# Layer 0's scores of two key tiles taken together: four float32 products, then the four float32r position products

## The chip, the cores and the metric

The kernel runs on one core of a Trainium2 chip. Its engines are TensorE (PE in the profile; its weight loads are shown apart as PEld), VectorE (DVE), ScalarE (ACT), GpSimd (POOL) and SyncE (SP, which only issues DMAs). Each works through its own instructions in the order in which they stand in its queue, and waits for the others through semaphores. The metric is the device time in microseconds of one execution.

## The reference, cut to what matters

Eight images of 32 x 32 points with 384 channels go through two layers. Layer 0 is an attention over the 1024 points of an image, with 6 heads of 64 channels and with positions relative in height and width added to the scores; layer 1 is a causal attention with one head of 384 channels and a feed-forward part with binarized weights. The change touches the scores of layer 0:

```python
attn = jnp.einsum('bqd,bkd->bqk', q * SCALE, k)
rel_h = jnp.einsum('bhwc,hkc->bhwk', r_q, Rh)
rel_w = jnp.einsum('bhwc,wkc->bhwk', r_q, Rw)
attn = attn.reshape(b * NH, h, w, h, w) + rel_h[:, :, :, :, None] + rel_w[:, :, :, None, :]
attn = attn.reshape(b * NH, hw, hw)
attn = jax.nn.softmax(attn, axis=-1)
out = jnp.einsum('bqk,bkd->bqd', attn, v)
...
return out @ proj_w + proj_b
```

## The kernel before

The images are worked through one after another (`ORDER`; one of the three images without a feed-forward part comes first). For an image, layer 0 makes queries, keys and values and tables of relative positions; `attend0_fast` does the attention; layer 1 follows, and in five of the eight images the feed-forward part.

In `attend0_fast` the loop runs over the 3 head pairs `p` and the 2 halves of 512 queries: 6 groups an image, 48 in all. A group goes over 8 tiles of 128 keys. The two heads of a pair (`par` 0 and 1) lie on partitions 0 to 63 and 64 to 127, so that their products use different halves of the array's rows.

- `scores(p, c, half)` takes one key tile: for each head a float32 product of keys and queries (L909) starts the sum in a PSUM bank, and a float32r product of a pattern of ones (`unit`) with the positions `r` (L913) ends it. First come the two heads' L909, then the two heads' L913. Then ScalarE takes the exponential of each bank (L920) into a page `pr0`, both heads side by side.
- A plain float32 product shows in the trace as two records, a float32r one as one; so L909 has 1536 records for 768 products, L913 768 for 768.
- `add_up` sums the eight pages of a group on VectorE (L925 for the first two, L927 for the rest); `values` multiplies probabilities and values on TensorE (L935), both heads into one bank on different columns of the array; ScalarE copies that bank to `oT` (L1007) except in the last group.
- `over_tiles` reduces the sums (L944, L946, the tile `few`). In most groups the totals then go through a DMA (`gathered`, L954 and L958) and come back a group later, where `reciprocals` takes them (L974, L976). In an image's last group (and in the first image's last two) `reciprocals` adds up across partitions with a small product on TensorE (L969) at once. What follows for the last group: L976, `widened` (L983, L984), the scaling of `oT` (L1017 for the group before, L1020 for the last one), and the projections (L1026, then L524).
- After the first half of a head pair, `later(p + 1, ...)` prepares the positions of the next one: two casts on ScalarE (L784) queued behind the group's last exponential, two subtractions on VectorE (L794) behind the last sum, and DMAs into `r` (L800) from SyncE and GpSimd.

What sets the order: instructions are placed by a scheduler that keeps data dependences and, among ready ones, mostly the order of the program. `behind_last()` puts each call's products behind `last_matmul`, the last product of the call before, on TensorE's queue; it makes no engine wait for another. A score tile is one of the 8 PSUM banks of the pool `ps_o`, taken in turn: a bank is free again when the exponential that reads it is done. Pages come from a pool of 12. L829 puts the last values of layer 0 in place before the first group of an image and L1362 is the first product of the feed-forward part.

Of the kernel before, what the change touches and what calls it, by code (L numbers as in the profile page):

```python
# [14 lines left out]
AF = mybir.ActivationFunctionType  # L15
# [4 lines left out]
P = 128  # L20
B, H, W, C = 8, 32, 32, 384
T = H * W
NJ = T // P
# [68 lines left out]
def conv_attn_hybrid(  # L92
# [19 lines left out]
    nc = tc.nc  # L112
# [144 lines left out]
    unit = const.tile([P, 2, HB, WB], F32R, name="unit")  # L257
# [51 lines left out]
    def layer1_forms(pools, raw, s):  # L309
        weight_forms(pools, nc.gpsimd, raw[:, ts(s, NC * C)].rearrange("p (k o) -> p k o", k=NC), s, w1f)  # L310
# [110 lines left out]
    def stages(pools):  # L421
# [151 lines left out]
        def behind_of(ins):  # L573
            return contextlib.nullcontext() if ins is None else tc.issue_after(ins)
# [318 lines left out]
        def attend0_fast(residual, b, q, k, r, v, later):  # L893
# [4 lines left out]
            rows = (slice(0, HD), slice(HD, P))  # L898
            last_exp, last_matmul, last_few = [None], [None], [None]

            def behind_last():
                return tc.issue_after(last_matmul[0]) if last_matmul[0] is not None else contextlib.nullcontext()

            def scores(p, c, half):

                sc = [pools.o_tile(f"s0_{b}_{p}_{c}_{half}_{par}") for par in range(2)]
                with behind_last():
                    for par in range(2):
                        nc.tensor.matmul(  # L909
                            sc[par], k[rows[par], p, ts(c, P)], q[rows[par], p, ts(half, 512)], start=True, stop=False  # L910
                        )
                    for par in range(2):
                        last_matmul[0] = nc.tensor.matmul(  # L913
                            sc[par], unit[rows[par], c // 2 % 2].rearrange("i h w -> i (h w)"),
                            r(2 * (c // 4) + c % 2, p)[rows[par], ts(half, 512)], start=False, stop=True,
                        ).ins
                pr = pools.page(f"pr0_{b}_{p}_{c}_{half}")
                for par in range(2):
                    with behind_of(exp_loaded[0]):
                        last_exp[0] = nc.scalar.activation(pr[:, ts(par, 512)], sc[par], AF.Exp).ins  # L920
                return pr

            def add_up(p, half, prs):
                total = pools.page(f"sum0_{b}_{p}_{half}")
                adds = [nc.vector.tensor_tensor(total, prs[0], prs[1], ALU.add).ins]  # L925
                for pr in prs[2:]:
                    adds.append(nc.vector.tensor_tensor(total, total, pr, ALU.add).ins)  # L927
                return total, adds

            def values(p, half, prs):  # L930
                av = pools.o_tile(f"av0_{b}_{p}_{half}")
                with behind_last():
                    for c, pr in enumerate(prs):
                        for par in range(2):
                            last_matmul[0] = nc.tensor.matmul(  # L935
                                av[ts(par, HD), :], v[:, c, ts(2 * p + par, HD)], pr[:, ts(par, 512)],
                                start=(c == 0), stop=(c == NJ - 1),
                            ).ins
                return av

            def over_tiles(p, half, total):

                tr = pools.page(f"tr0_{b}_{p}_{half}")
                nc.vector.transpose(tr, total)  # L944
                few = pools.small.tile([P, 2, 16], F32, tag="few", bufs=2, name=f"few_{b}_{p}_{half}")
                last_few[0] = nc.vector.tensor_reduce(  # L946
                    few, tr.rearrange("p (a n i) -> p a n i", a=2, i=32), AX.X, ALU.add
                ).ins
                return few

            def gathered(p, half, few):

                kept = store.tile([P, 32], F32, tag="few", bufs=2, name=f"{pools.path}_few_{b}_{p}_{half}")
                nc.sync.dma_start(out=kept, in_=few.rearrange("p a n -> p (a n)"))  # L954
                parts = pools.small.tile([P, 4, 16], F32, tag="parts", bufs=2, name=f"parts_{b}_{p}_{half}")
                at = kept[0:1, 0:1]
                for i in range(4):
                    nc.sync.dma_start(  # L958
                        out=parts[ts(i, 32)],
                        in_=bass.AP(at.tensor, at.offset + i // 2 * 16, [[32, 32], [32 * 32, 4], [1, 16]]),  # L960
                    )
                return parts

            def reciprocals(p, half, few, parts=None):
                if parts is None:
                    den = pools.o_tile(f"den0_{b}_{p}_{half}")[:, :16]
                    with behind_last():
                        for par in range(2):
                            last_matmul[0] = nc.tensor.matmul(  # L969
                                den[ts(par, HD)], fold.rearrange("p a i -> p (a i)"), few[:, par, :], start=True, stop=True  # L970
                            ).ins
                else:
                    den = pools.small.tile([P, 16], F32, tag="den0", bufs=2, name=f"den0_{b}_{p}_{half}")
                    nc.vector.tensor_reduce(den, parts.rearrange("p a n -> p n a"), AX.X, ALU.add)  # L974
                rt = pools.small.tile([P, 16], F32, tag="rt0", bufs=2, name=f"rt0_{b}_{p}_{half}")
                nc.vector.reciprocal(rt, den)  # L976
                check(den, rt, b * PER_IMAGE + 2 * p + half)
                return rt

            def widened(p, half, rt):  # L980
                room = pools.page(f"wide0_{b}_{p}_{half}")
                wide, rb = room[:, :512], room[:, 512:]
                nc.vector.tensor_copy(wide.rearrange("p (n i) -> p n i", i=32), rt.unsqueeze(2).to_broadcast([P, 16, 32]))  # L983
                nc.vector.transpose(rb, wide)  # L984
                return rb

            xt, waiting = None, None
            for p, half in itertools.product(range(NPAIR), range(2)):
                t, last = ts(half, 512), (p, half) == (NPAIR - 1, 1)
                prs = [scores(p, c, half) for c in range(NJ)]  # L990
                if b == ORDER[0] and (p, half) == (0, 0):
                    with tc.issue_after(last_row[0]):
                        layer1_forms(pools, raw1[0], 1)
                if b == ORDER[0] and (p, half) == (2, 0):
                    signs.append(binarize(pools))
                    next(signs[0])
                total, adds = add_up(p, half, prs)
                if waiting is not None:
                    p0, t0 = waiting[0], ts(waiting[1], 512)
                    with tc.issue_after(adds[4 if last else 5]):  # L1000
                        rt = reciprocals(*waiting)
                    if not last:
                        rb = widened(p0, waiting[1], rt)
                        nc.gpsimd.tensor_tensor(oT[:, p0, t0], oT[:, p0, t0], rb, ALU.mult)
                av = values(p, half, prs)
                if not last:
                    nc.scalar.copy(oT[:, p, t], av)  # L1007
                if (p, half) == (1, 0):
                    xt = residual()
                if half == 0 and p + 1 < NPAIR:  # L1010
                    later(p + 1, last_exp[0], adds[-1])
                few = over_tiles(p, half, total)
                at_once = last or (b == ORDER[0] and p == NPAIR - 1)
                if last:
                    with tc.issue_after(last_few[0]):
                        rb = widened(p0, waiting[1], rt)
                    nc.vector.tensor_tensor(oT[:, p0, t0], oT[:, p0, t0], rb, ALU.mult)  # L1017
                waiting = (p, half, few, None if at_once else gathered(p, half, few))
# [522 lines left out]
    with ExitStack() as scope:  # L1541
        pools = Pools(scope, tc, "f")
# [42 lines left out]
```

## Time and profile before

| what | value |
|---|---|
| median of the runs | 2267.55 us (2267.29 to 2268.35, 3 runs) |
| the profiled execution | 2271.02 us |
| its span, first to last instruction | 2269.2 us |
| granted clock of TensorE, mean | 0.999 |
| L909 MATMUL, float32 scores | 1536 records, busy 400.6 us |
| L913 MATMUL, float32r positions | 768 records, busy 310.0 us |
| L920, exponentials on ScalarE | 768, busy 412.4 us, mean 595 ns |
| L925 and L927, sums on VectorE | 336, busy 430.2 us |
| L935 MATMUL, values | 1536 records, busy 340.2 us |

The ends of products in the trace are modelled, and a product that is issued early shows a long record; the busy times of L909 and L913 therefore overlap. What a product costs is better read from the distance between starts, or from the chain of waits, in which each stretch of time is given to one line. Shares of the span in that chain: L909 15%, L935 15%, L913 4%.

### The profile page before, as it was taken

To read this page: it belongs to the slowest core of one execution; us is meant where nothing else is said; L and a number is where in the kernel's file an instruction comes from. 1 tells how busy PE (TensorE), PEld (TensorE's weight loads), DVE (VectorE), ACT (ScalarE), POOL (GpSimd) and SP (SyncE) were. 2 spreads that over 40 slices of the span, in tenths; PEclk is the share of its full clock that TensorE was granted. 3 is DMA by queue.
4 is the path that set the end of the run, shared out by engine and by line. 5 is a ranking of instruction groups with operands and counts; after the bars stand their busy time and mean duration, and the time that the engine had idled before them with its cause. 6 is when DMAs were issued, how large, how long until landed. Compare 5 with 4: busy or idle time off the path is not lost.

```text
span 2269.2 us, 30149 instructions
## 1 busy us (share of the span) xinstructions
PE 2257.0 (99%) x10597; PEld 1387.8 (61%) x10597; DVE 1633.2 (72%) x2746; ACT 1208.3 (53%) x2181; POOL 527.2 (23%) x696
## 2 busy tenths in 40 slices
PE   9999999999999999999999999999999999999998
PEld 4547554768645677547685475874477754755475
DVE  6898578875888548886468884588864788727882
ACT  4654266337664457654476543767444766317541
POOL 7512222230131401312102313013040131221310
PEclk9999999999999999999999999999999999999999
DMA  6530562140740205520308202074102372016200
GB/s 192 146 93 28 159 139 55 47 163 29 150 104 29 73 40 120 127 65 1 112 30 186 67 29 108 21 153 111 31 5 107 73 170 60 10 47 153 56 1 30
DMA packets 182048, 188.50 MB, mean 83 GB/s; under 512 B 138763, under 2 KB 151488, under 8 KB 179072
## 3 DMA queue, kind: packets, MB, share of 16 engines
q1 hardware_dynamic: 163680, 115.80, 20.9%
q0 software_dynamic: 17376, 69.30, 9.8%
q8 instruction: 87, 1.43, 0.3%
q10 hardware_dynamic: 832, 1.38, 0.2%
q14 instruction: 73, 0.60, 0.1%
HBM read 84.52 MB, written 51.56 MB: 60 GB/s over the span
## 4 chain that ended last, share of the span: by engine, by line
PE 99%; DVE 0%; DMA 0%; SPq 0%; issue 0%; ACT 0%
PE f_s L909 15%; PE f_av L935 15%; PE f_av L1218 8%; PE f_s L1204 8%; PE f_y L1412 7%; PE f_y L1362 7%; PE f_qk L578 6%; PE f_s L913 4%; PE f_pr_A L578 4%; PE f_pr_B L578 3%; PE f_pj L1026 3%; PE f_pj L524 3%; PE f_rel L578 2%; PE f_pr_1v_A L578 2%; PE f_pr_1q_A L578 2%; PE f_pr_1v_B L578 2%
## 5 line engine op out<-in xcount | busy, mean ns | idle before, releaser
L920 ACT ACTIVATE f_pr<-f_s 128x512 f32<-128x512 f32 x768 | 412.4, 595 | 40.8 <-PE f_s L913 36.3
L909 PE MATMUL f_s<-f_q,f_k 64*128 64x512 f32 x1536 | 400.6, 595 | 2.4 <-DVE f_v L829 2.4
L927 DVE TENSOR_TENSOR f_sum<-f_sum,f_pr 128x1024 f32<-128x1024 f32 x288 | 368.0, 1278 | 25.9
L935 PE MATMUL f_av<-f_pr,f_v 128*64 128x512 f32 x1536 | 340.2, 595 | 0.0
L913 PE MATMUL f_s<-f_r,unit 64*128 64x512 f32 x768 | 310.0, 792 | 0.0
L935 PEld LDWEIGHTS f_av<-f_pr,f_v 128*64 128x64 f32 x1536 | 106.0, 137 | 218.3 <-issue 191.9
L909 PEld LDWEIGHTS f_s<-f_q,f_k 64*128 64x128 f32 x1536 | 148.0, 186 | 127.0 <-issue 66.5
L1204 PE MATMUL f_s<-f_q,f_lnT 128*128 128x512 f32 (+3 forms) x576 | 198.3, 488 | 0.0
L1218 PE MATMUL f_av<-f_v,f_pr 128*128 128x385 f32 (+1 forms) x576 | 195.4, 486 | 0.0
L800 POOL DMA_DIRECT2D f_r<-f_far x192 | 102.2, 535 | 389.9 <-DVE f_far L794 175.7
L1218 PEld LDWEIGHTS f_av<-f_v,f_pr 128*128 128x128 f32 x576 | 108.1, 190 | 77.0 <-issue 11.5
L1213 ACT ACTIVATE f_pr<-f_s 128x512 f32<-128x512 f32 (+3 forms) x96 | 47.0, 491 | 203.1 <-DVE f_s L1209 160.2
L1204 PEld LDWEIGHTS f_s<-f_q,f_lnT 128*128 128x128 f32 x576 | 100.7, 190 | 70.0 <-issue 46.9
L1373 DVE TENSOR_REDUCE am<-f_h 128x1 f32<-128x1024 f32 (+2 forms) x80 | 71.6, 946 | 95.6 <-ACT f_h L1366 95.6
L1366 ACT ACTIVATE f_h<-f_y,biases 128x256 f32<-128x256 f32 x240 | 100.8, 471 | 66.8 <-PE f_y L1362 66.8
L913 PEld LDWEIGHTS f_s<-f_r,unit 64*128 64x128 f32 x768 | 76.3, 187 | 88.7 <-issue 88.5
L578 PE MATMUL f_qk<-f_gnT,wq_sb 128*128 128x512 f32 x288 | 127.9, 595 | 0.0
L1412 PE MATMUL f_y<-f_w2a,f_hilo 128*128 128x384 f32 x640 | 127.2, 341 | 0.0
L1007 ACT COPY f_oT<-f_av 128x512 f32<-128x512 f32 x40 | 23.5, 587 | 190.4 <-PE f_av L935 190.4
L1412 PEld LDWEIGHTS f_y<-f_w2a,f_hilo 128*128 128x128 f32 x640 | 112.5, 188 | 3.8 <-issue 1.4
L925 DVE TENSOR_TENSOR f_sum<-f_pr,f_pr 128x1024 f32<-128x1024 f32 x48 | 62.2, 1295 | 71.8 <-ACT f_pr L920 71.8
L1316 POOL PARTITION_ALL_REDUCE qa<-qg x10 | 3.7, 367 | 459.1 <-DVE qg L1314 459.1
(286 smaller groups left out, 4189.2 us busy)
## 6 DMA issues: line engine op xcount, KB each, us to landing
f_far<-f_far SPq DMA_DIRECT2D x48, 512.0 KB, 4.6
f_r<-f_far SPq DMA_DIRECT2D x192, 128.0 KB, 3.0
f_r<-f_far POOLq DMA_DIRECT2D x192, 128.0 KB, 4.5
f_far<-f_far SPq DMA_DIRECT2D x192, 64.0 KB, 4.7
f_x<-in_x SPq DMA_DIRECT2D x32, 384.0 KB, 4.7
f_gnT<-in_xT SPq DMA_DIRECT2D x21, 512.0 KB, 4.8
f_w1a<-w1s POOLq DMA_DIRECT2D x5, 1536.0 KB, 6.6
f_w2a<-w2s POOLq DMA_DIRECT2D x5, 1536.0 KB, 8.2
```

Of the source, the lines that this page charges most:

```text
L578: last_product[0] = nc.tensor.matmul(*args, **kw).ins
L800: put = (nc.gpsimd if i else nc.sync).dma_start(out=r(part, p).bitcast(F32).rearrange("(m i) t -> i m t", i=4)[2 * i + d], in_=pages[i][ts ...
L909: nc.tensor.matmul(sc[par], k[rows[par], p, ts(c, P)], q[rows[par], p, ts(half, 512)], start=True, stop=False)
L913: last_matmul[0] = nc.tensor.matmul(sc[par], unit[rows[par], c // 2 % 2].rearrange("i h w -> i (h w)"), r(2 * (c // 4) + c % 2, p)[rows[pa ...
L920: last_exp[0] = nc.scalar.activation(pr[:, ts(par, 512)], sc[par], AF.Exp).ins
L927: adds.append(nc.vector.tensor_tensor(total, total, pr, ALU.add).ins)
L935: last_matmul[0] = nc.tensor.matmul(av[ts(par, HD), :], v[:, c, ts(2 * p + par, HD)], pr[:, ts(par, 512)], start=(c == 0), stop=(c == NJ - 1),
L1204: last_score[0] = nc.tensor.matmul(sc[:, lo:], xT[:, c // 4, k, ts(c % 4, P)], q[:, half, k, lo:], start=(k == 0), stop=(k == NC - 1),).ins
L1218: made = nc.tensor.matmul(av, prs[c][:, ts(j - c, P)], what(c), start=(c == 0), stop=(c == j)).ins
L1362: nc.tensor.matmul(ps, w1k[i // 2][:, ts(m, P)], xs[i % 2][:, half, i // 2, :], start=(i == 0), stop=(i == 2 * NC - 1))
L1366: nc.scalar.activation(pairs[i][:, m, :, :], ps[:, ts(i % 2, 256)].rearrange("p (j q) -> p j q", j=2), AF.Identity, bias=b1_sb[:, m : m + 1],)
L1412: nc.tensor.matmul(ps[:, :C], h, w, start=(i == 0), stop=(i == len(products) - 1))
```

## The change

`scores` takes two key tiles at a time. It issues the float32 products of both tiles and both heads, then the float32r products of both, then the four exponentials in the order in which they stood before. Banks, pages and exponentials are the same in number and order; the products of one pair of tiles stand in another order on TensorE's queue, and a pair's four banks and two pages are asked for together.

```diff
-            def scores(p, c, half):
+            def scores(p, cs, half):
-                sc = [pools.o_tile(f"s0_{b}_{p}_{c}_{half}_{par}") for par in range(2)]
+                sc = {(c, par): pools.o_tile(f"s0_{b}_{p}_{c}_{half}_{par}") for c in cs for par in range(2)}
                 with behind_last():
-                    for par in range(2):
+                    for c, par in sc:
                         nc.tensor.matmul(
-                            sc[par], k[rows[par], p, ts(c, P)], q[rows[par], p, ts(half, 512)], start=True, stop=False
+                            sc[c, par], k[rows[par], p, ts(c, P)], q[rows[par], p, ts(half, 512)], start=True, stop=False
                         )
-                    for par in range(2):
+                    for c, par in sc:
                         last_matmul[0] = nc.tensor.matmul(
-                            sc[par], unit[rows[par], c // 2 % 2].rearrange("i h w -> i (h w)"),
+                            sc[c, par], unit[rows[par], c // 2 % 2].rearrange("i h w -> i (h w)"),
                             r(2 * (c // 4) + c % 2, p)[rows[par], ts(half, 512)], start=False, stop=True,
                         ).ins
-                pr = pools.page(f"pr0_{b}_{p}_{c}_{half}")
-                for par in range(2):
+                prs = [pools.page(f"pr0_{b}_{p}_{c}_{half}") for c in cs]
+                for c, par in sc:
                     with behind_of(exp_loaded[0]):
-                        last_exp[0] = nc.scalar.activation(pr[:, ts(par, 512)], sc[par], AF.Exp).ins
-                return pr
+                        last_exp[0] = nc.scalar.activation(prs[c - cs[0]][:, ts(par, 512)], sc[c, par], AF.Exp).ins
+                return prs
...
-                prs = [scores(p, c, half) for c in range(NJ)]
+                prs = [pr for c in range(0, NJ, 2) for pr in scores(p, (c, c + 1), half)]
```

## The prediction

> **What bounds the kernel now.** I read the page first: busy shares and the chain that ended last.
>
> ```profile
> PE 2257.0 (99%) x10597; PEld 1387.8 (61%) x10597; DVE 1633.2 (72%) x2746; ACT 1208.3 (53%) x2181; POOL 527.2 (23%) x696
> PE 99%; DVE 0%; DMA 0%; SPq 0%; issue 0%; ACT 0%
> L920 ACT ACTIVATE f_pr<-f_s 128x512 f32<-128x512 f32 x768 | 412.4, 595 | 40.8 <-PE f_s L913 36.3
> ```
>
> TensorE (PE) is the chain from end to end, so only two things count: how long a product holds the array, and whether the array is ever made to wait. The exponentials (L920) wait for TensorE, not the reverse. Next I read the chain of waits in order of time, at the end of a scores group (image 0, last head pair and half) and in the first feed-forward product of the same image; the columns are start, length, what, and how many records. A plain float32 product is two records.
>
> ```profile
> 384.73 1.06 PE f_s L909 x4
> 385.79 0.23 PE f_s L913 x2
> 386.01 0.86 PE f_s L909 x4
> 386.87 0.23 PE f_s L913 x2
> ...
> 393.64 0.57 PE f_av L935
> ```
>
> ```profile
> 500.90 5.28 PE f_y L1362 x23
> ```
>
> One key tile costs 0.86 us for its two float32 products (the two heads lie on different halves of the array's rows and run side by side) and 0.23 us for its two float32r products: 1.09 us, 8 times a group. The start of a group costs 0.20 us more once (1.06 against 0.86), its end the 0.57. All this is TensorE time; nothing else shows in it. The L1362 line is a run of float32r products alone, one after the other with new weights each: 5.28/23 = 0.230 us each.
>
> Last, the VectorE timeline around the end of that image's attention, and what its tile few releases:
>
> ```profile
> 388.26 1.22 DVE L925 TENSOR_TENSOR f_sum<-f_pr,f_pr 128x1024 f32<-128x1024 f32 x1 [3.18 <-ACT f_pr L920]
> 389.58 5.21 DVE L927 TENSOR_TENSOR f_sum<-f_sum,f_pr 128x1024 f32<-128x1024 f32 x4
> ...
> 398.80 1.22 DVE L946 TENSOR_REDUCE few<-f_tr 128x32 f32<-128x1024 f32 x1
> 399.93 0.42 DVE L983 COPY f_wide<-rt 128x512 f32<-128x512 f32 x1
> 400.78 0.26 DVE L976 RECIPROCAL rt<-f_den 128x16 f32<-128x16 f32 x1 [0.43 <-PE f_den L969]
> ```
>
> VectorE idles until the exponentials of the first two key tiles are there (388.26, which is 3.60 us after the group's start at 384.66), then runs without a gap to the end of L946 at 400.02. TensorE takes few into the product L969 at 400.49. So this side path arrives 0.47 us before it is needed: the one short cover that I find.
>
> **What the skill says.** "TensorE: Matmul & The Clock Gate", section "Back-to-back issue gap", gives N/2.4 + 2.5 ns for an isolated product, 216 ns for 512 columns; "FP8 and Floating Point Precision", section "TensorE Precision Notes", gives true float32 four passes. The trace agrees for float32: successive records of one head are 429 ns apart, 858 for a product, four times 214.5. It does not for float32r: 230 to 232 ns. "TensorEngine Tiling (Array Packing)", section "Key Properties", says that a change of tiling mode drains the array. That fits the 0.20 us at a group's start, after L935's other tiling; float32 and float32r within a group have the same tiling, so it gives the change nothing to save. The first page's "The mechanism" says that a weight load overlaps running products only where the row group differs. The trace says otherwise: in L1362, where all use all rows, a load starts 2 to 3 ns after the product before it.
>
> **The change, part by part.**
>
> (1) Nothing is added or removed: 1536 float32 records, 768 float32r products, 768 exponentials, same tiles in the same order from the same pools. Only TensorE's order changes: per pair of key tiles f f r r f f r r (f, r: one head's product) becomes f f f f r r r r. There are 8 images x 3 head pairs x 2 halves x 4 = 192 pairs in 48 groups.
>
> (2) TensorE's rate. Per pair the old order has two steps from r to f, the new one a step r to r and a step r to f; and one f after f in place of an f after r. What would be saved is the price of switching. Averaged over the starts of all groups but the first, a key tile takes 1090.2 ns; less two times 429 that leaves 232.4 ns for a float32r product with float32 on both sides. L1362's 715 steps of float32r after float32r average 232.1 ns. The surplus over 216 is thus the product's own, not the switch's: saving 0.3 ns x 192 = 0.06 us, nothing. That f after f costs 429 as elsewhere I take from records 1 and 2 of a product, which also have different weights. Unseen is r after r with 64 rows. From below it can't beat 214.5 (a float32 pass): -18 ns x 192 = -3.4 us. From above its weight load is not hidden: a group's first load shows that price, first to second record 534 ns against 429, so +105 ns x 192 = +20 us. I take 232 because loads of both row groups start together behind a running product in every step of the old order, and 232 ns is enough for them.
>
> (3) Banks. Each of 8 PSUM banks is taken again by the tile 8 later, two pairs on. A pair's first exponential can start 2.25 us after the pair does (step 4), the four follow at 0.49 us (379 of the steps from one exponential to the next are 490 to 499 ns; those of about 595 are TensorE's pace), each lasts 0.59. The fourth frees its bank at about 4.3 us; its successor is needed at 2 x 2.18 + 0.86 = 5.2 us. Cover 0.9 us; no stall. Four exponentials at 0.49 are 1.96 us, below the pair's 2.18, so ScalarE doesn't fall behind.
>
> (4) When the first exponentials come. Old: second float32 record at 0.534 us, its float32r record ends 0.818 later, the exponential 0.036 after that: 1.39 us. New: two more float32 records go in front, 2 x 0.429, so 2.25 us. VectorE's first sum needs the fourth exponential. Old start 3.60 us. New: 2.25 + 3 x 0.49 + 0.59 + 0.03 = 4.34, taken as 0.75 later (0.70 to 0.81 with spacings of 0.478 to 0.494 and up to 0.09 more at the start). In an image's other groups it is hidden: the result goes through a DMA and is used a group later, and where VectorE is already behind (first sum 4.4 to 6.6 us after the group's start) it isn't late at all.
>
> (5) What is late next. In the last group of each image the 0.75 uses up the 0.47 of cover (0.47 to 0.49 in seven images, 0.61 in the first one run). With 0.06 us from VectorE's end to TensorE's start (as at 70.41 to 70.47, L829 to L909) L969 waits 0.75 + 0.06 - 0.48 = 0.33 us. Behind it on TensorE's queue are the projections L1026, which can't pass it: 7 x 0.33 + 0.20 = +2.5 us. Further down nothing more is lost: the later pieces of L1026 need L1017, done at 402.33 for 403.35, and L1020, done at 404.2 for 408.5; both shift with TensorE up to the remaining 0.45.
>
> (6) Moved past other queues. The casts L784 behind the last exponential and their DMAs L800 come about 0.65 us later. Where a later head pair needs them they landed 3.8 to 7.7 us early. In an image's first group they land up to 3.5 us after its start, and the new order asks for them later, not earlier. Semaphore instructions ahead of L913 (192, so 8 for each of the 24 groups that first use a head pair's positions) are about 0.11 us apart and fall in a running pass; uncovered, two of them would be 0.22 us x 24 groups = 5 us at the worst, I take 0. In the first group of the run, which stalls on VectorE's L829 at 67.45 to 70.47, waiting for two more banks may add 0.1 to 0.3.
>
> Sum: 0 + 2.5 = +2.5 us on a span of 2269.2. The profiled run took 2271.02, with 1.8 us around the span; the median of the runs shown is 3.5 below it. I put the difference on the median: 2267.55 + 2.5 = 2270.0.
>
> **The rivals.** "Same" means within 0.2%, 4.5 us, about what a measurement of this kernel can tell from no change.
> A, the forecast: 2270.0, own range 2267.5 to 2272 (chance 0.50, of it 0.03 above 2272.1).
> B, switching has a price that a full-array run conceals: against it stand 232.4 and 232.1; for it that only wide-array runs could be compared. At 214.5 for r after r: -3.4 + 2.5, so 2266.6 (0.10, same). If more than half of the surplus of a pair over bare passes goes (2180 against 10 x 214.5 = 2145 ns, so up to 35 ns, -6.7 us, and the wait of step 5 stays away): 2261 to 2263 (0.13, faster).
> C, the slower side: the second float32r product's weights are loaded late[...]. +105 ns a pair at full price: 2267.55 + 20.2 + 2.5 = 2290; it decides from (4.5 - 2.5)/192 = 10 ns a pair (0.12). Against it: the old order hides such loads behind passes of 232 ns.
> D, exponentials four in a row keep 0.595, not 0.49: the first sum is then 1.07 late, and step 5 costs 0.65 x 8 = 5 us: 2272.7 (0.10, slower).
> E, the order of issue doesn't change, since the instruction order is made by a scheduler that may put a ready float32r product ahead of a float32 product whose bank isn't free: 2267.6 (0.05).
>
> **How the numbers follow.** The likeliest is A. Faster 0.13 (B's part); slower 0.03 + 0.12 + 0.10 = 0.25; same 0.62. The range leaves out C's upper part and B's lower end: 2263.5 to 2276.
>
> **What would show it.** Right: the chain reads about 1.72 for eight L909 records and 0.46 for four L913; the first L925 of a last group starts 4.3 us after the group; L969 begins 0.06 after L946's end and TensorE's gap ahead of it grows by 0.3. Wrong: 0.43 or less, or 0.55 and more, for four L913 records; a waiting L909 inside a group; a first sum at 4.6 or later.

## The result and the profile after

| | before | after |
|---|---|---|
| median of 13 runs each, same chip | 2267.55 us (2267.22 to 2268.71) | 2272.6 us (2272.02 to 2273.38) |
| ratio, 95% interval | | 1.0023 [1.0015, 1.003] |
| profiled execution, span | 2271.02, 2269.2 | 2272.55, 2270.8 |

The change costs 5.05 us. The two profiled executions differ by 1.5 us only, because the one of before held a stall of its own (so did those of the first, fourth and fifth experiment below): a second profile of the unchanged kernel took 2267.55 with a span of 2265.8 and has no stall at L829. Below, "before" in a comparison of traces is that second profile; its span and the one of after differ by 5.0 us.

First the page of the kernel after, the lines that answer to those of before:

```profile
PE 2258.2 (99%) x10597; PEld 1383.0 (61%) x10597; DVE 1636.3 (72%) x2746; ACT 1192.2 (53%) x2181; POOL 529.2 (23%) x696
PE 94%; DVE 4%; issue 1%; ACT 1%; DMA 0%; SPq 0%; DVEq 0%
L920 ACT ACTIVATE f_pr<-f_s 128x512 f32<-128x512 f32 x768 | 397.0, 603 | 93.7 <-PE f_s L913 79.4
```

Busy times and counts hardly move. The chain does: VectorE had 0% of it and now has 4%, with 1% each for ScalarE and for time that nothing shown explains. So there are stretches in which TensorE is no longer what everything waits for. ScalarE waits longer for TensorE (93.7 for 40.8 us), since its exponentials now come in bursts of four; of what waits for ScalarE because of that, only the first sum of an image's last group will matter (VectorE's L927 waits 5.5 us more in all, most of it in images' first groups, at no cost to TensorE).

The chain of waits of the kernel after, inside an ordinary group of image 0 (start, length, what, records):

```profile
365.63 1.92 PE f_s L909 x8
367.55 0.47 PE f_s L913 x4
368.02 1.72 PE f_s L909 x8
369.73 0.47 PE f_s L913 x4
370.20 1.72 PE f_s L909 x8
371.92 0.46 PE f_s L913 x4
```

Here the time per product is what it was: 1.72 for eight L909 records, 0.46 to 0.47 for four L913. From a group's first L909 to the first L935 it took 8.924 us before and 8.928 after (medians over 48 groups). The new order saves nothing and costs nothing on the array.

The same chain of after at the end of that image's attention, which no longer runs over the scores at all:

```profile
385.90 1.23 DVE f_sum L925
...
395.26 1.16 DVE f_tr L944
396.42 0.03 issue
396.45 1.23 DVE few L946
397.68 0.04 issue
397.72 0.29 PE f_den L969 x4
398.01 4.07 PE f_pj L1026 x12
```

And the VectorE timeline there, then the two lines of TensorE that matter, the start of the group and L969 (in brackets the idle time before it and what ended it):

```profile
385.90 1.22 DVE L925 TENSOR_TENSOR f_sum<-f_pr,f_pr 128x1024 f32<-128x1024 f32 x1 [3.19 <-ACT f_pr L920]
387.23 5.21 DVE L927 TENSOR_TENSOR f_sum<-f_sum,f_pr 128x1024 f32<-128x1024 f32 x4
...
396.45 1.22 DVE L946 TENSOR_REDUCE few<-f_tr 128x32 f32<-128x1024 f32 x1
```

```profile
381.50 1.99 PE L909 MATMUL f_s<-f_q,f_k 64*128 64x512 f32 x8
...
397.72 0.29 PE L969 MATMUL f_den<-few,fold 128*64 128x16 f32 x4 [0.20 <-DVE few L946]
```

The two lines that answer to the last ones, in the second profile of before:

```profile
395.53 1.22 DVE L946 TENSOR_REDUCE few<-f_tr 128x32 f32<-128x1024 f32 x1
```

```profile
397.22 0.24 PE L969 MATMUL f_den<-few,fold 128*64 128x16 f32 x4
```

In the trace of after this group starts at 381.50, so the first sum begins 4.40 us in (3.60 before), and VectorE then works without a gap to the end of L946. L969 starts 54 ns after that end; before it started 468 ns after. That holds in all eight images (54 or 55 ns in each). The view of waits puts only 0.2 us per image to it (1.4 us over 7 images), because the modelled ends of L935 cover part of the gap; starts are the better measure. From the first L935 of the last group to L969 it now takes 0.365 to 0.377 us more in seven images and 0.233 in the first one run, 2.83 together. From L969 to L1026 it takes 0.05 more in each: the second half of L969 follows 72 ns behind the first where it was 21. Sum 3.23 us.

The other 1.8 us lie elsewhere. SyncE's last instructions, by their source line in the profile of after and in the second one of before (count, shortest, median and longest in ns, first and last start):

```profile
L1581 SPq EVENT_SEMAPHORE  x14: 17/28/28, 2268.1 to 2270.8; - x14
```

```profile
L1581 SPq EVENT_SEMAPHORE  x14: 17/28/28, 2264.2 to 2265.8; - x14
```

The same 14 instructions take 2.7 us where they took 1.6. The records show one gap of 1.09 us between two of them, at 2268.52. The page's list of DMA queues differs in one line, first after, then before:

```profile
q14 instruction: 74, 0.61, 0.1%
```

```profile
q14 instruction: 73, 0.60, 0.1%
```

One fetch of instructions more falls within the span. That doesn't show that SyncE waited for it: in the packets of after it starts at 2270.26, when the gap is over, and in before the same last fetch starts at 2267.37, when the span is over.

SyncE has 1107 instructions in the trace of after, 1095 before, and all of the difference is separate semaphore waits: 10 for 22 ahead of L441, 62 for 53 ahead of L769, 114 for 99 ahead of L800. They aren't new. Both traces have 30149 instructions in all; against SyncE's twelve waits more, ScalarE has 8 fewer, GpSimd 3 and VectorE 1, and ScalarE's own have moved too (41 for 13 ahead of L1213). None of VectorE's, ScalarE's or SyncE's operations has changed place (one GpSimd addition, L888, has moved past one multiplication); what moved is where the separate waits stand.

Of the rest, 0.44 us are small steps of both signs in TensorE's starts between one image's attention and the next one's, most of them in the layer 1 projections and the feed-forward part. Another 0.33 us is SyncE's wait ahead of the 14 instructions (3.21 us for 2.88); in the traces with 1095 instructions below it takes 2.94 to 3.19, so this part is the luck of the two executions. What is left over comes to -0.1 us.

### The profile page after: what moved, and what is told of

The parts are those of the page before. It is cut to its first block, busy times and chain, and to the rows that moved or that the text cites. A ratio compares the mean times of both kernels' runs of the same rounds, so it can differ in the third digit from the quotient of the medians.

```text
span 2270.8 us, 30149 instructions
## 1 busy us (share of the span) xinstructions
PE 2258.2 (99%) x10597; PEld 1383.0 (61%) x10597; DVE 1636.3 (72%) x2746; ACT 1192.2 (53%) x2181; POOL 529.2 (23%) x696
## 4 chain that ended last, share of the span: by engine, by line
PE 94%; DVE 4%; issue 1%; ACT 1%; DMA 0%; SPq 0%; DVEq 0%
PE f_s L909 13%; PE f_av L935 12%; PE f_av L1218 8%; PE f_s L1204 8%; PE f_y L1412 7%; PE f_y L1362 7%; PE f_qk L578 6%; PE f_pr_A L578 4%; PE f_s L913 3%; PE f_pr_B L578 3%; PE f_pj L1026 3%; PE f_pj L524 3%; DVE f_sum L927 2%; PE f_rel L578 2%; PE f_pr_1v_A L578 2%; PE f_pr_1q_A L578 2%
## 5 line engine op out<-in xcount | busy, mean ns | idle before, releaser
L920 ACT ACTIVATE f_pr<-f_s 128x512 f32<-128x512 f32 x768 | 397.0, 603 | 93.7 <-PE f_s L913 79.4
L927 DVE TENSOR_TENSOR f_sum<-f_sum,f_pr 128x1024 f32<-128x1024 f32 x288 | 369.3, 1282 | 31.2 <-ACT f_pr L920 5.5
L909 PE MATMUL f_s<-f_q,f_k 64*128 64x512 f32 x1536 | 367.7, 595 | 0.0
L935 PE MATMUL f_av<-f_pr,f_v 128*64 128x512 f32 x1536 | 340.2, 595 | 0.0
L935 PEld LDWEIGHTS f_av<-f_pr,f_v 128*64 128x64 f32 x1536 | 106.0, 137 | 209.0 <-issue 191.9
L909 PEld LDWEIGHTS f_s<-f_q,f_k 64*128 64x128 f32 x1536 | 143.7, 186 | 135.9 <-issue 121.5
L913 PE MATMUL f_s<-f_r,unit 64*128 64x512 f32 x768 | 202.6, 600 | 0.0
L800 POOL DMA_DIRECT2D f_r<-f_far x192 | 102.0, 534 | 391.1 <-DVE f_far L794 177.6
L1213 ACT ACTIVATE f_pr<-f_s 128x512 f32<-128x512 f32 (+3 forms) x96 | 47.0, 490 | 202.6 <-DVE f_s L1209 159.7
L913 PEld LDWEIGHTS f_s<-f_r,unit 64*128 64x128 f32 x768 | 74.3, 187 | 90.5 <-issue 90.0
L1390 DVE SCALAR_TENSOR_TENSOR f_hilo<-f_h,f_hilo 128x768 fp32r<-128x768 f32 (+1 forms) x85 | 77.2, 909 | 44.7 <-ACT f_h L1389 44.7
```

The costliest lines, as they stand in the source:

```text
L800: put = (nc.gpsimd if i else nc.sync).dma_start(out=r(part, p).bitcast(F32).rearrange("(m i) t -> i m t", i=4)[2 * i + d], in_=pages[i][ts ...
L909: nc.tensor.matmul(sc[c, par], k[rows[par], p, ts(c, P)], q[rows[par], p, ts(half, 512)], start=True, stop=False)
L913: last_matmul[0] = nc.tensor.matmul(sc[c, par], unit[rows[par], c // 2 % 2].rearrange("i h w -> i (h w)"), r(2 * (c // 4) + c % 2, p)[rows ...
L920: last_exp[0] = nc.scalar.activation(prs[c - cs[0]][:, ts(par, 512)], sc[c, par], AF.Exp).ins
L935: last_matmul[0] = nc.tensor.matmul(av[ts(par, HD), :], v[:, c, ts(2 * p + par, HD)], pr[:, ts(par, 512)], start=(c == 0), stop=(c == NJ - 1),
```

## The experiments

Each run has a kernel before beside it on its chip: 2267.21 for the first three below, 2267.42 for the next four, 2267.48 and 2267.68 for the last two. Every kernel does the whole computation; only orders differ, and in the last one eight small loads are added. Where pairs are taken, `scores` is that of the change; the diffs show only what chooses the pairs, or are cut with `...`.

**Pairs everywhere except in an image's last group.**

```diff
-                prs = [pr for c in range(0, NJ, 2) for pr in scores(p, (c, c + 1), half)]
+                pairs = [(c,) for c in range(NJ)] if last else [(c, c + 1) for c in range(0, NJ, 2)]
+                prs = [pr for cs in pairs for pr in scores(p, cs, half)]
```

> Pairs of key tiles everywhere except in an image's last group, which has the old order. Theory (the loss is L969's wait for few): L969 starts 6.92 us after the first L935 of the last group again, the waits of 0.37 us (8 of them, 3.2 us with what follows them) are gone, time about 2269.4. Rival (the loss is spread over all pairs, a dearer product or load): 7/48 to 8/48 of the 5.05 us come back, time about 2271.8.

Measured: 2267.67 us, ratio 1.0003 [0.9994, 1.0011]. With 152 of 192 pairs in the new order (160 by the edit, but the first pair of each image's first group keeps the old one, see E below) there is no loss and no gain within the interval, which runs from -1.4 to 2.5 us. So all or nearly all of the 5 us hangs on the last groups, the 1.8 us too, which the expectation had left standing.

**Only the first pair of an image's last group.**

```diff
+                pairs = [(0, 1)] + [(c,) for c in range(2, NJ)] if last else [(c,) for c in range(NJ)]
```

> The old order everywhere, but for the first two key tiles of an image's last group: 8 pairs of 192. Theory (what counts is when the first sum on VectorE can start): first sum 4.40 us after the group's start, L969 waits as after the change, +3 us, time about 2270.6. Rival (spread over pairs): 8/192 of 5.05, +0.2 us, time 2267.8.

Measured: 2270.67, ratio 1.0014 [1.0008, 1.0021], +3.46 us from 8 pairs. L969 is late by 0.37 to 0.39 (first image 0.235), about as with the change, and L1026 by 0.05 more: 3.28 in the trace. SyncE has 1095 instructions here and no gap at its end.

**The change in full, with L969 behind the first projection product.**

```diff
...
+            def multiply(*jks):
...
+            multiply((0, (0,)))
             rb = widened(p, half, reciprocals(*waiting))
             nc.vector.tensor_tensor(oT[:, p, t], av, rb, ALU.mult)
...
-                for j, ks in ((0, (0, 1)), (1, (0, 1)), (0, (2,)), (1, (2,)), (2, (0, 1, 2)), (3, (0, 1, 2))):
+            multiply((0, (1,)), (1, (0, 1)), (0, (2,)), (1, (2,)), (2, (0, 1, 2)), (3, (0, 1, 2)))
```

`multiply` issues the projection products L1026 (L1025 here) that it is told; `widened(...)` holds L969.

> The change in full, but L969 is issued behind the first product of the projection (0.65 us) in place of ahead of it. Theory (TensorE stands still for few): the wait is covered, no stop at L969, 3.2 us come back, time about 2269.4. Rival (spread over pairs): stays at 2272.6.

Measured: 2271.98, ratio 1.002 [1.0012, 1.0028]. A miss: the wait is gone, since L969 now starts 0.62 to 0.63 us after few (0.76 in the first image), but only 0.6 us came back, nearer to the rival's number than to the theory's. The next run takes the same move alone.

**The same move in the kernel before.**

> The old order of the scores everywhere; only L969 stands behind the first projection product instead of ahead of it. Here no wait for few exists, so only the price of the move shows. Theory (the array changes its tiling twice more: about 0.10 us ahead of the projection product, 0.105 us of a weight load that nothing hides, 0.09 us and the change back ahead of L969): 0.35 us in each of 8 images, +2.8 us, 2270.0 to 2270.4. Rival (the first order's loss lies further down VectorE's chain, so moving L969 costs nothing in itself): 2267.2 to 2267.6.

Measured: 2270.1, ratio 1.0011 [1.0005, 1.0018], +2.7 us where nothing had to wait, as expected. The chain of waits in this kernel, image 0:

```profile
397.51 0.84 PE f_pj L1025 x2
398.36 0.22 PE f_den L969 x4
398.58 3.42 PE f_pj L1025 x10
```

Together 4.48 us. The chain of after has 4.07 for the same twelve projection records; with the 0.07 that L969 takes in the chain of before that is 4.14. The move itself costs 0.34 to 0.35 per image, 2.79 in the trace. This fits the Trainium skill, "TensorEngine Tiling (Array Packing)", section "Key Properties": a change of tiling mode drains the array. Here the move makes two more changes, to the projection's tiling (128\*128) and back to that of L935 and L969 (128\*64), and has that price. How much of it is the change of tiling and how much a weight load that nothing hides, no run here separates. The cure cost as much as the illness.

**Only the last pair of the last group.**

```diff
+                pairs = [(c,) for c in range(6)] + [(6, 7)] if last else [(c,) for c in range(NJ)]
```

> The old order everywhere, only key tiles 6 and 7 of an image's last group taken together: 8 pairs, as many as in the run with the first pair. Theory (only the first sum's start counts): first sum at 3.60 us, few in time, L969 does not wait, 2267.2 to 2267.6. Two points could bring a little: the exponentials of tile 6 come about 0.75 us later, which VectorE's sums, being behind, do not notice. Rival (each pair taken together at the end of an image costs 0.43 us, wherever it stands): 2270.7.

Measured: 2269.28, ratio 1.0009 [1.0001, 1.0017]. Both theories miss. First sum at 3.6 us, few 474 ns early in image 0, no wait for it anywhere, as the theory says, and still +1.86. What this kernel shares with the full change is the other arrangement of waits: 1107 SyncE instructions and a gap of 1.35 us among SyncE's last ones, which take 3.0 us:

```profile
L1582 SPq EVENT_SEMAPHORE  x14: 17/28/28, 2265.9 to 2268.9; - x14
```

So it measures the second loss alone, though roughly: the interval runs from 0.2 to 3.9 us.

**The last group's first two key tiles single, the other six in pairs.**

```diff
+                pairs = [(0,), (1,), (2, 3), (4, 5), (6, 7)] if last else [(c,) for c in range(NJ)]
```

> The old order everywhere, in an image's last group the key tiles 0 and 1 alone, then 2 and 3, 4 and 5, 6 and 7 together: 24 pairs. Theory: the first sum begins at 3.60 us as before, but the second must wait for the exponentials of tile 2, about 0.62 us; few comes 0.62 later, L969 waits 0.62 + 0.05 - 0.48 = 0.2 us in 7 images and hardly in the first, with what lies between L969 and L1026 +1.9 us: 2269.1. Rival by the number of pairs (0.43 us each): +10 us, 2277. Rival that only the first sum counts: 2267.5.

Measured: 2271.61, ratio 1.0019 [1.0012, 1.0027]. The VectorE timeline of this kernel:

```profile
385.11 1.23 DVE L925 TENSOR_TENSOR f_sum<-f_pr,f_pr 128x1024 f32<-128x1024 f32 x1 [3.17 <-ACT f_pr L920]
387.12 5.21 DVE L927 TENSOR_TENSOR f_sum<-f_sum,f_pr 128x1024 f32<-128x1024 f32 x4 [0.78 <-ACT f_pr L920]
```

The first sum is on time; the second begins 2.01 us after it, where 1.33 was usual (385.90 and 387.23 in the timeline of after), so 0.68 late for the 0.62 worked out. L969 is late by 0.24 to 0.27 in seven images (0.115 in the first one run) and L1026 by 0.05 more: 2.31 in the trace. The rest of the 4.19 is again the arrangement with 1107 instructions. The expectation missed that part.

**Three key tiles together at the start of the last group.**

```diff
+                pairs = [(0, 1, 2)] + [(c,) for c in range(3, NJ)] if last else [(c,) for c in range(NJ)]
```

> The old order everywhere, in an image's last group the first three key tiles taken together: six float32 products, then six float32r. Theory: two float32 products more ahead of the first exponential, so the first sum comes about 1.6 us later than before, at 5.2 us; less 0.48 of cover, with 0.06 of semaphore L969 waits 1.15 us in 7 images and 1.0 in the first, about +9.5 us: 2276.8. Rival (the loss of the one pair is a fixed price for the change of order): 2270.7, as with one pair.

Measured: 2277.49, ratio 1.0044 [1.003, 1.0058], +10.07. TensorE's line for L969 in this kernel:

```profile
399.39 0.29 PE L969 MATMUL f_den<-few,fold 128*64 128x16 f32 x4 [1.06 <-DVE few L946]
```

The first sum comes at 5.26. The loss follows the delay of the first sum, not the number of changes in order: 1.66 us of delay for 0.80, less the same cover, gives three times the loss (10.11 in the trace for 3.28 with one pair).

**The change in full, except for the last pair of the last group.**

```diff
+                pairs = [(c, c + 1) for c in range(0, NJ, 2)]
+                if last:
+                    pairs[3:] = [(6,), (7,)]
```

> The change in full, except that in an image's last group the key tiles 6 and 7 stay single. Theory of two terms (the wait at L969 costs 3.25 us; the program's separate waits fall into another arrangement, 1107 SyncE instructions for 1095, only when that last pair is taken together, and this costs 1.86 us by the run that takes only that pair): first sum at 4.35 to 4.40, L969 late as with the change, but 1095 SyncE instructions, no 1.1 us gap at the end: 2267.4 + 3.3 = 2270.7. Rival (the 1.8 us come from the 192 pairs themselves): 2272.4, for 184 of them are there.

Measured: 2270.79, ratio 1.0013 [1.0007, 1.002]. The sum of two terms, put down beforehand, was good to 0.1 us: 1095 instructions, L969 late as with the change, and no gap, since SyncE's last 14 take 1.6 us:

```profile
L1584 SPq EVENT_SEMAPHORE  x14: 17/28/28, 2267.5 to 2269.1; - x14
```

**Eight small DMAs more on SyncE, in the kernel before.**

```diff
+            for n in range(0 if spared else 8):
+                spared.append(nc.sync.dma_start(out=spare[:1, ts(n, 8)], in_=proj_b[ts(n, 8)].partition_broadcast(1)))
```

> The kernel before with eight DMAs of 32 bytes more on SyncE, once, in a stretch where its queue waits for VectorE; they load a tile that nobody reads. Only SyncE's instruction count matters here: 1095 + 8 or some more, which is past the 1097 after which every run with 74 fetches of q14 stood still at the end. Theory (the gap at the end is a fetch of SyncE's next instructions, due to its number of instructions alone): a gap of 1.0 to 1.35 us after SyncE's 1097th instruction, 74 fetches, 2268.5 to 2268.9. Rival (the gap and the rest come from where the waits stand): no gap, 2267.4; bounds for the eight DMAs themselves -0.1 to +0.3.

Measured: 2268.57, ratio 1.0001 [0.9993, 1.0009]. That is 0.89 us over its kernel before and within the theory's numbers, but the interval is too wide to settle 1 us. The trace does. The queue line and SyncE's last instructions in this kernel:

```profile
q14 instruction: 74, 0.61, 0.1%
```

```profile
L1584 SPq EVENT_SEMAPHORE  x14: 17/28/28, 2264.1 to 2266.9; - x14
```

These 14 instructions again take 2.8 us. SyncE has 1103 instructions, and it stands still for 1.18 us after the 1097th, as after the 1097th in the change and in the three experiments with 1107. With 1095 it never gets there. It isn't one wait that comes late either: after the change the eighth of the 14 is held up, here the twelfth. TensorE's starts, but for one shift of all by 0.25 us to earlier, stay where they were within some 20 ns from the scores of the first image to the end, so here it is SyncE's end alone. The span is 1.13 us longer. The count of instructions is thus shown to bring the gap. That a fetch is what SyncE waits for, as the expectation has it, is not: in all five kernels with the gap the last fetch ahead of its end had landed 0.9 us or more before SyncE went on, and the 74th starts only later.

What the two terms give, us over the kernel before of the same chip:

| kernel | late at L969, from the trace | arrangement, 1.86 where SyncE has 1107 | sum | measured |
|---|---|---|---|---|
| pairs except in last groups | 0 | 0 | 0 | 0.46 |
| first pair only | 3.28 | 0 | 3.28 | 3.46 |
| change, L969 moved | 2.79 (the move) | 1.86 | 4.65 | 4.77 |
| before, L969 moved | 2.79 (the move) | 0 | 2.79 | 2.68 |
| last pair only | 0 | 1.86 (taken from here) | 1.86 | 1.86 |
| two single, then pairs | 2.31 | 1.86 | 4.17 | 4.19 |
| three together | 10.11 | 0 | 10.11 | 10.07 |
| change but the last pair | 3.27 | 0 | 3.27 | 3.31 |
| the change | 3.23 | 1.86 | 5.09 | 5.05 |

The traces bear the second term out, at 1.4 to 1.8 us: the gap of 1.0 to 1.35, and 0.43 to 0.47 us that TensorE loses between the images' attentions in each of the four kernels with 1107 instructions (stops of a single execution left out). In those with 1095 TensorE loses nothing there (-0.11 to -0.04).

## Why the prediction was right, and where it was short

The direction, and the place and mechanism of the larger part, were right, and 2272.6 lies in the range of 2263.5 to 2276; the forecast of 2270.0 was 2.6 us short, half of the loss. That is beyond the forecast's own range of 2267.5 to 2272, and the change lies just past the prediction's line of 0.2% for "same", to which it had given 0.62; the interval of the ratio includes that line. The range reached above 2272 for the sake of C and D, of which neither happened, so that it holds the result is partly luck.

- Steps 1 and 2, nothing saved on TensorE: right. Four float32r products in a row take 0.46 to 0.47, the forecast 0.46; groups are equal within 5 ns. The rivals of cheaper switching (B) and of an unhidden weight load (C) fall with it: 5 ns in a group are about 1 ns a pair, where C was to decide from 10 ns on. The time of the run without the last groups agrees, but its interval alone would not exclude 10 ns.
- Step 3, banks: right, no L909 waits inside a group.
- Step 4, first sum at 4.34: it came at 4.40 in the last groups. (By the step's own terms the delay could reach 0.84, not 0.81.) D needed 4.6 or later and is refuted, although its 2272.7 is the number that was measured. The time alone could not have told the two apart.
- Step 5, L969 and L1026 late: the mechanism is shown by four runs (one pair, three tiles, two single, the change but its last pair). The size was short: 0.33 us in seven images were 0.37, since the first sum was 0.80 late and not 0.75; and the 0.05 between L969 and L1026 was not in the sum. Measured 3.23 for 2.5.
- Step 6, the other queues at nothing: this is the term that failed. Their order did not change, as it says, and the worst case it named, semaphores ahead of L913, did not happen. But the separate semaphore waits fell into another arrangement, twelve of them from other engines to SyncE, and this cost 1.86 us: 1.0 to 1.35 at SyncE's end, 0.43 to 0.47 on TensorE between the images' attentions. That only the last group's last pair brings it about is shown by the runs with and without that pair. How the pair leads to that arrangement was not tried, nor was TensorE's part, which eight more instructions on SyncE did not bring; what SyncE waits for in its gap isn't shown either. These stay open.
- E, an unchanged order: it happened only in the first pair of each image's first group, which kept its old order (first sum there at 3.60), so that 184 of the 192 pairs changed.
- The sum was put on the median because of the stall at L829: right, the second profile of before has none.

No version beat the kernel before. Pairs outside the last groups equal it within what can be measured.

## What to carry to other kernels

When products are moved ahead of others, ask who takes the first result of the group, not how fast the group is: here the array's time stayed the same and the loss came from one side path with 0.47 us of cover, 8 times. A reorder on one engine can change where waits stand on engines that it doesn't touch; before a difference of 1 or 2 us is explained by a mechanism, count each engine's instructions and semaphore waits in both traces. A cure that puts a product of another tiling in between has to be priced first.

## What the runs showed of the hardware

- SyncE stood still for 1.0 to 1.35 us at the end of the kernel in all five programs that gave it more than 1097 instructions in the trace (1107 in four, 1103 in one), always after that one; its other last instructions start mostly some 60 to 90 ns apart, and the end of the execution waits for them. The Trainium skill, "Runtime: NRT & Kernel Launch", section "Instruction fetch mechanics", says that engines fetch instructions block by block and that the cost of crossing into the next block is mostly hidden. A stop at a fixed count would fit a crossing that isn't hidden, but no run here shows it: no fetch was under way in the last 0.9 us of the stop.
- Float32r products on half of the array's rows, two at a time: the second two of four took the same 0.23 us (0.46 to 0.47 for the four) as two between float32 products.
- From the end of VectorE's L946 to the start of TensorE's waiting L969: 54 to 55 ns in all eight images after the change.
- Two changes of tiling more around one small product, in the kernel before: 0.34 to 0.35 us an image, what it does to weight loads included.
